# A graph layer whose one-hots get 128 columns: two columns of zeros, a later turning of fields, and parted sums of three rows

## The chip, the cores and the metric

The kernel runs on one core of one Trainium2 chip. The metric is the time of one execution on the device in microseconds (us). A core has five engines that run side by side and each take their instructions in order: PE (TensorE, the matmuls; its weight loads are shown as an engine of their own, PEld), DVE (VectorE), ACT (ScalarE), POOL (GpSimd, which also issues the gathers here) and SP (SyncE, which issues the plain DMAs).

## The reference

A graph with 625 nodes of 512 features and 20,625 edges, sorted by their destination, goes through one relational layer with four relations, and then through a feed-forward network:

```
h   = relu(layernorm(x))
msg = sum over r of (h[src] @ W_rel[r] + b_rel[r]) * where(edge_type == r, edge_weight, 0)
agg = segment_sum(msg, dst) / max(segment_sum(edge_weight, dst), 1)
x1  = layernorm(h + h @ W_self + b_self + agg) * g1 + b1
out = x + layernorm(x1 + gelu(x1 @ W_ffn1 + b_ffn1) @ W_ffn2 + b_ffn2) * g2 + b2
```

All inputs and the output are 32-bit floats; indices are 32-bit integers.

## The kernel before

The nodes are five blocks of 125 (`NG = 125`, padded to 128). The kernel has three stages.

**Table stage.** `table_rows(r, i)` makes one table row: block `i` of `h` times `W_rel[r]` (L366, four matmuls, each of which the profile shows as two records of 512 columns), scaled by ACT (L374) and written to a table in HBM by SP (L376). There are 4 x 5 = 20 such rows, in the order `(r, i)`, and 20 chunks of the table, so called. The last nine chunks (`KEPT = 9`) also stay in SBUF.

**Weights of dense blocks.** Three of the five blocks (`OUTER`) get their sums as a product: for each node of the block the edge weights are summed over (relation, source node), which gives a matrix `sums_w`, and this is multiplied with the table (L1043, one matmul for each of 20 chunks and each block; chunks that didn't stay come back from HBM as tiles `tr`, L1038). A node has up to 64 slots for edges. The slots' fields are turned by PE (`turn_fields`, L597) and copied by ACT (L600). They are taken in 12 units of 16 slots (`units`: 3 blocks x 4). For a unit, `slot_hots` makes one-hots on DVE: `low` (L614; which of the 125 source rows, and one more column that is always one), `eq` (L617) and three `high` (L620; which chunk, times the weight split in three bf16 parts). `slot_sums` then makes a *bank*: for each of four slots PE loads a piece of `low` as weights and multiplies it with a piece of `high` of 120 columns (L631). `empty_sums` (DVE, L637) adds the three parts of a bank into `sums_w`. So a unit is four banks, and all is 48 banks, or 192 weight loads and matmuls.

In memory `low` is laid out with the index of the slot inside (`TB = 8`), so that neighbouring columns of one weight load lie eight bf16 elements, 16 bytes, apart.

The first units are handled between the table rows: from a row given in the loop a unit is taken whenever few banks are waiting (`EARLY` units in all), and up to three banks (`PER_ROW`) are put behind each later table row. These rows are emitted in a fixed order by hand.

**Gather stage.** The rest is ordered by a planner (`Plan`): every operation has an engine, an estimated duration, what it comes after, buffers that it takes and gives back, and a rank; the planner plays this through and emits the instructions in the order it finds, so each engine's order is fixed when the kernel is built. In this stage are the units that are left, the products with the table, `h @ W_self` (L386), and the edges of the two blocks that aren't dense: POOL gathers 69 tiles of 128 table rows (L919, eight buffers `ms`) and four more (L973), with a pause behind every fourth (L915). Three gathered tiles make one sum: ACT writes the first, weighted, into a PSUM bank (L925; two banks, `add`), DVE adds the second and the third (L943). Then PE multiplies it with a one-hot. A *whole* sum does this with one 32-bit matmul (L966, two records). A *parted* sum is split into two halves of a shorter format, the high half by ACT (L929) and the low half by DVE (L933), and takes two short matmuls (L963, L964). Which sums are parted is said by

```
PARTED = 1, 2
def parted(k, units):
    return k % PARTED[1] < PARTED[0] and k + 3 < len(units)
```

so before it is every second one, except near the end of a group of sums.

**Tail.** Each block is normalised, turned (L319) and put through the feed-forward network (L714 up, L732 down); three blocks come last.

Of the kernel before, what the change touches and what calls it, by code (L numbers as in the profile page):

```python
# [12 lines left out]
BF16 = mybir.dt.bfloat16  # L13
# [3 lines left out]
P = 128  # L17
# [119 lines left out]
def gnn_layer(ctx, tc, x, edges, edge_groups, firsts, fourths, windows, w_self, w_rel, w_ffn1, w_ffn2, brel_in, rows_in, bf1_in, out, n_edges):  # L137
# [12 lines left out]
    nc = tc.nc  # L150
# [10 lines left out]
    NG = ep.each  # L161
# [7 lines left out]
    SL = windows.shape[1] // 4  # L169
# [11 lines left out]
    mid = ctx.enter_context(tc.tile_pool(name="mid", bufs=1))  # L181
# [89 lines left out]
    TB = 8  # L271
    TP = 2
# [1 line left out]
    grid = mid.tile([P, NG, TB], BF16, name="grid")  # L274
    keys = mid.tile([P, 2 * NC, TP], BF16, name="keys")
    ident_b = early.tile([P, P], BF16, name="ident_b")
    lows = [mid.tile([P, SL // 4 // TB, NG + 1, TB], BF16, name=f"low_{n}") for n in range(2)]

    def node_constants():
        place = early.tile([P, 1], F32, name="place")  # L280
        nc.gpsimd.iota(place, pattern=[[0, 1]], base=0, channel_multiplier=1, allow_small_or_imprecise_dtypes=True)
        nc.gpsimd.memset(node_f, 2.0 * N)
        nc.gpsimd.memset(xw, -1.0)
        for b in range(NB):
            n = ep.size[b]
            nc.vector.tensor_scalar(node_f[:n, at_of[b]:at_of[b] + 1], place[:n], float(ep.first[b]), None, op0=ALU.add)
            if b in inner:
                nc.vector.tensor_scalar(xw[:n, 0, b - B0:b - B0 + 1], place[:n], float(b * P), None, op0=ALU.add)
        nc.gpsimd.iota(keys, pattern=[[1, 2 * NC], [0, TP]], base=0, channel_multiplier=0,
                       allow_small_or_imprecise_dtypes=True)  # L290
        for t in lows:
            nc.gpsimd.memset(t[:, :, NG:, :], 1.0)
        nc.gpsimd.iota(grid, pattern=[[1, NG], [0, TB]], base=0, channel_multiplier=0,
                       allow_small_or_imprecise_dtypes=True)

# [37 lines left out]
    def pre_norm(i, mean):  # L333
        for c in (slice(0, D // 2), slice(D // 2, D)) if i == 0 else (slice(0, D),):
            nc.vector.tensor_scalar(z[:, i, c], xs[:, i, c], mean, 0.0, op0=ALU.subtract, op1=ALU.max)
        nc.vector.tensor_scalar(rx[:, i, 0:1], var_of[i], EPS, None, op0=ALU.add)
        rsqrt_pow(rx[:, i, :])
# [3 lines left out]
    def x_stats(i):  # L341
        st = work.tile([P, 2 if i == 0 else 1, 6], F32, tag="bn", name=f"st_x{i}", bufs=HOTS)
        w = D // st.shape[1]
        for h in range(st.shape[1]):
            nc.vector.bn_stats(st[:, h, :], xs[:, i, h * w:(h + 1) * w])
        mv = work.tile([P, 2], F32, tag="mv", name=f"mv_x{i}", bufs=HOTS)
        nc.vector.bn_aggr(mv, st)
        var_of[i] = mv[:, 1:2]
        return mv[:, 0:1]
# [240 lines left out]
    QT = 4  # L590
    UNIT = SL // 4
# [31 lines left out]
    def slot_sums(d, u, q, low, high, place):  # L623
        if (d, u, q) == (d, 0, 0):
            sums_w[OUTER[d]] = const.tile([P, NC, P], F32, tag="sums_w", name=f"sums_w{d}", bufs=2)
        pool, tag = place
        p = pool.tile([P, D], F32, tag=tag, name=f"bank_{d}_{u}_{q}")
        W = 3 * 2 * NC
        for i in range(QT):
            t = q * QT + i  # L630
            nc.tensor.matmul(p[:NG + 1, i * W:(i + 1) * W], low[:, t // TB, :, t % TB], high[:, t // TP, :, t % TP],  # L631
                             start=True, stop=True)
        return p

# [160 lines left out]
    PAUSE = 200  # L795
    RUN = 4
    LATER = 0.3
    PARTED = 1, 2
    LA = 3
    CH = 2  # L800
    FIRST_AT = (2, 3)
    units = [(d, u) for d in range(ND) for u in range(SL // UNIT)]
    EARLY = 7
    PER_ROW = 3
    with tc.manual_schedule(engines={PE, DVE, ACT, mybir.EngineType.Pool}):
        nc.scalar.activation(gelu_of, ones, AF.Gelu)
        node_constants()
        stats = x_stats(0)

        def next_norm(i):  # L810
            nonlocal stats
            if i < NB:
                pre_norm(i, stats)
            if i + 1 < NB:
                stats = x_stats(i + 1)

        warm = ps_one.tile([P, D], F32, tag="one", name="warm")
        for _ in range(WARM):
            nc.tensor.matmul(warm, zeros[:, :P], zeros, start=True, stop=True)
        next_norm(0)  # L820
        for k, n in ((0, 1), (1, 1), (2, 2)):
            transposed(hT[0][:, k:k + n, :], z[:, 0, k * P:(k + n) * P], f"h0_{k}")
        next_norm(1)
        hots, waiting, later, sums_now = {}, units[:EARLY], [], []
        for r in range(R):
            for i in range(NB):
                def next_transposed():
                    transposed(hT[i + 1], z[:, i + 1, :], f"h{i + 1}")
                    next_norm(i + 2 if i == 0 else i + 3)

                table_rows(r, i, next_transposed if r == 0 and i + 1 < NB else None)
                for d, u, q in sums_now:
                    p = slot_sums(d, u, q, *hots[d, u], ((ps_one, "one"), (ps_acc, "acc"), (ps_add, "add"), (ps_add, "add"))[q % 4])
                    empty_sums(d, u, q, p)
                sums_now = [later.pop(0) for _ in range(min(PER_ROW, len(later)))]
                if r == 0 and i < 3:
                    if i == 0:
                        next_norm(3)
                        find_tiles()
                    rows_of_tiles(2 * i, min(2 * i + 2, NB))  # L840
                if (r, i) == (0, 3):
                    find_windows()
                if (r, i) == (1, 0):
                    edge_columns()
                if (r, i) == (1, 1):
                    slot_weights(0, ND)
                    slot_fields()
                if (r, i) == (1, 4):
                    slot_weights(ND, NB)
                    slot_degrees()  # L850
                    degrees_turned = relation_degrees()
                if (r, i) == (2, 2):
                    degrees_turned()
                if (r, i) >= (1, 3) and waiting and len(later) + len(sums_now) <= UNIT // QT:
                    d, u = waiting.pop(0)
                    if d not in turned_fields:
                        turn_fields(d)
                    hots[d, u] = slot_hots(d, u)
                    later += [(d, u, q) for q in range(UNIT // QT)]
                if (r, i) == (1, NB - 1):  # L860
                    group_columns()
                if r == 3 and i < KD:
                    nc.vector.tensor_add(ws_sb[:, i, i * P:(i + 1) * P], ws_sb[:, i, i * P:(i + 1) * P], ident)
                if (r, i) == (3, 0):
                    for g_bc in (g1_bc, g2_bc):
                        nc.vector.tensor_scalar(g_bc, g_bc, 1.0 / RS, None, op0=ALU.mult)
                if (r, i) == FIRST_AT:
                    first_edges()
                    load_first_edges()
                if (r, i) == (2, NB - 1):  # L870
                    set_limits(0)
                    set_limits(1)
                    total_outside = count_outside()
            later_loads(r)
        assert not waiting
        for d, u, q in sums_now + later:
            p = slot_sums(d, u, q, *hots[d, u], ((ps_one, "one"), (ps_acc, "acc"), (ps_add, "add"), (ps_add, "add"))[q % 4])
            empty_sums(d, u, q, p)
        for d in range(ND):
            if d not in turned_fields:  # L880
                turn_fields(d)
# [53 lines left out]
    def parted(k, units):  # L935
        return k % PARTED[1] < PARTED[0] and k + 3 < len(units)

# [45 lines left out]
    g_last, g_before, n = None, None, 0  # L983
# [62 lines left out]
    m, ld, t, here = {b: None for b in OUTER}, None, None, {}  # L1046
    summed, h, e = {}, None, None

    def weights_of(d):
        nonlocal h, e  # L1050
        for i, (dd, u) in enumerate(units):
            if dd != d or i < EARLY:
                continue
# [12 lines left out]
    stay, i = list(range(NC - KEPT, NC)), 0  # L1066
    for d, b in enumerate(OUTER):
        weights_of(d)
        order = (*stay, *range(NC - KEPT)) if d != 1 else (*range(NC - KEPT), *stay)
        for c in order:  # L1070
            if c not in stay and (b, c) not in here:
                n = min(CH, NC - KEPT - c)
# [8 lines left out]
            if i == 8:  # L1081
                t = op("PE", 0.1, lambda: total_outside(), after=[m[b], first_ready], take=["ps"], give=["ps"], lag=2.0, rank=(2, 2.085))
# [15 lines left out]
    for b in range(NB):  # L1098
# [3 lines left out]
        for name, eng, us, fn, needs in steps:  # L1102
# [4 lines left out]
        p = [None]  # L1107
        t = op("PE", 0.46, lambda got=got, p=p, b=b: p.__setitem__(0, turn(got["x1"], f"x1_{b}")),
               after=[made["x1"]], take=["ps"], give=["ow"], rank=(1,))
# [5 lines left out]
    for blocks in together:  # L1115
        members, n = [], 0
# [177 lines left out]
```

## Time and profile before

| | before |
|---|---|
| time, median of 3 runs | 303.15 us (300.43 to 304.28) |
| profiled execution: time | 304.07 us |
| profiled execution: span of the trace | 302.2 us |
| mean granted TensorE clock | 0.977 |
| PE busy | 283.5 us (94%) |
| DVE busy | 188.5 us (62%) |
| POOL busy | 102.3 us (34%) |
| ACT busy | 60.1 us (20%) |
| moved by DMA | 47.94 MB |

The span runs from the first to the last instruction of the core, and the time of an execution has a little around it: 304.07 - 302.2 = 1.87 us here. Busy times are of the engine itself. A "group" of instructions is those of one line, engine, operation and shape, with their busy time and the mean of one in nanoseconds, and behind the bar the idle time of the engine just before them and what ended it. The chain is the work that ended last, followed back from the end; its pieces are exclusive, so that pieces on PE in a row give PE's true pace.

### The profile page before, as it was taken

What the parts mean: (1) busy time and instruction counts of PE and PEld (TensorE: products, weight loads), DVE (VectorE), ACT (ScalarE), POOL (GpSimd) and SP (SyncE); (2) the same over time, 40 slices, a digit from 0 to 9 for tenths busy, and PEclk for the clock granted to TensorE, in tenths of its full rate; (3) what the DMA queues carried; (4) which work ended last, traced back from release to release, by engine and by line L of the source; (5) the groups of instructions that cost most, each with busy time, mean ns of one, the idle gap of its engine ahead of it and who ended that gap; (6) DMA issues with size and microseconds to landing.
All of it is one profiled execution on the core that took longest, in us unless ns stands there. A gap on an engine that the chain in (4) does not pass through costs nothing.

```text
span 302.2 us, 3190 instructions
## 1 busy us (share of the span) xinstructions
PE 283.5 (94%) x1047; PEld 174.3 (58%) x1047; DVE 188.5 (62%) x440; ACT 60.1 (20%) x115; POOL 102.3 (34%) x146
## 2 busy tenths in 40 slices
PE   7999949999999999999697979999999999999991
PEld 3444414776677575644263745685954456686870
DVE  5613179677594678974686739697979650650614
ACT  2331120111210020212021202032532001121230
POOL 6161500000300008777777474742777110000000
PEclk9999987999999999999999979999999999999997
DMA  7759765852111139668999998551567332001011
GB/s 236 293 150 342 252 210 216 313 206 63 39 36 50 49 110 282 176 170 221 297 258 291 286 257 242 150 170 35 152 193 196 120 100 72 2 0 34 2 36 37
DMA packets 19972, 47.94 MB, mean 159 GB/s; under 512 B 2351, under 2 KB 3065, under 8 KB 19824
## 3 DMA queue, kind: packets, MB, share of 16 engines
q1 hardware_dynamic: 13348, 27.54, 28.1%
q0 software_dynamic: 6304, 19.89, 23.2%
q10 hardware_dynamic: 300, 0.26, 0.4%
q8 instruction: 9, 0.15, 0.2%
q14 instruction: 11, 0.09, 0.1%
HBM read 41.29 MB, written 6.52 MB: 158 GB/s over the span
## 4 chain that ended last, share of the span: by engine, by line
PE 73%; DMA 12%; DVE 6%; issue 4%; POOL 3%; SPq 1%; DVEq 0%; POOLq 0%
PE acc L1043 14%; PE pt L366 14%; PE bank L631 12%; PE pu L714 12%; PE po L732 11%; PE pz L386 5%; DMA tr<-table 4%; DMA ms<-table,row_i 4%; PE acc L966 3%; DMA xs<-in_x_dram 2%; DMA win<-in_windows_dram,at_i 2%; POOL dst L462 2%; PE acc L960 1%; POOL win L462 1%; PE acc L964 1%
## 5 line engine op out<-in xcount | busy, mean ns | idle before, releaser
L919 POOL DMA_INDIRECT ms<-table,row_i x69 | 69.0, 1000 | 70.6 <-DVE eq L617 33.7
L366 PE MATMUL pt<-wr,hT 128*128 128x512 f32 x160 | 74.4, 614 | 0.2
L631 PEld LDWEIGHTS <-low 128*126 128x126 bf16 x192 | 48.5, 321 | 9.9 <-issue 6.4
L637 DVE TENSOR_REDUCE sums_w<-bank 126x160 f32<-126x480 f32 x48 | 31.2, 656 | 30.7 <-PE bank L631 30.7
L366 PEld LDWEIGHTS pt<-wr,hT 128*128 128x128 f32 x160 | 30.3, 197 | 33.3 <-issue 32.8
L631 PE MATMUL bank<-high,low 128*126 128x120 bf16 x192 | 44.3, 367 | 0.0
L714 PE MATMUL pu<-x1T,w_sb 128*128 128x125 f32 x320 | 37.8, 276 | 0.0
L714 PEld LDWEIGHTS pu<-x1T,w_sb 128*128 128x128 f32 x320 | 36.9, 192 | 1.4 <-issue 1.4
L1043 PE MATMUL acc<-tr,sums_w 126*128 126x512 f32 x66 | 32.7, 626 | 3.7 <-DMA tr<-table 3.7
L732 PE MATMUL po<-w_sb,gT 128*125 128x512 f32 (+2 forms) x96 | 35.7, 521 | 0.0
L925 ACT ACTIVATE ea<-ms,ed 128x512 f32<-128x512 f32 x23 | 15.9, 691 | 60.6 <-DMA ms<-table,row_i 33.4
L943 DVE SCALAR_TENSOR_TENSOR ea<-ms,wgt_g,ea 128x512 f32<-128x512 f32 x31 | 22.9, 747 | 8.0 <-DMA ms<-table,row_i 6.6
L374 ACT ACTIVATE m<-pt,rx 125x512 f32<-125x512 f32 x20 | 13.7, 687 | 70.5 <-PE pt L366 60.4
L732 PEld LDWEIGHTS po<-w_sb,gT 128*125 128x125 f32 x96 | 16.5, 188 | 15.2 <-issue 13.0
L1043 PE MATMUL acc<-m,sums_w 126*128 126x512 f32 x54 | 25.2, 596 | 0.0
L718 ACT ACTIVATE gT<-pu,bf 128x125 f32<-128x125 f32 x40 | 14.7, 366 | 46.2 <-PE pu L714 46.2
L1043 PEld LDWEIGHTS acc<-tr,sums_w 126*128 126x128 f32 x66 | 12.4, 199 | 16.3 <-issue 11.6
L740 DVE TENSOR_TENSOR y<-po,z 125x512 f32<-125x512 f32 (+2 forms) x6 | 3.6, 603 | 24.2 <-PE po L732 24.2
L386 PE MATMUL pz<-ws_sb,hT 128*128 128x512 f32 x40 | 18.1, 596 | 0.0
L1043 PEld LDWEIGHTS acc<-m,sums_w 126*128 126x128 f32 x54 | 10.0, 191 | 10.2 <-issue 10.1
L555 POOL DMA_INDIRECT x_edges<-in_edge_groups_dram,x_group x2 | 1.9, 944 | 41.2 <-DVE x_group L551 40.9
L620 DVE TENSOR_TENSOR high<-eq,turned 128x640 bf16<-128x640 bf16 x36 | 15.5, 487 | 0.4
(168 smaller groups left out, 243.2 us busy)
## 6 DMA issues: line engine op xcount, KB each, us to landing
tr<-table SPq DMA_DIRECT2D x15, 504.0 KB
table<-m SPq DMA_DIRECT2D x20, 250.0 KB
w_sb<-in_L_gnn_W_ffn_dram SPq DMA_DIRECT2D x2, 2048.0 KB
wr<-in_L_gnn_W_rel_dram SPq DMA_DIRECT2D x3, 1024.0 KB
rows<-in_rows_dram SPq DMA_DIRECT2D x1, 1536.0 KB
ms<-table,row_i POOLq DMA_INDIRECT x69, 4.1
ws_sb<-in_L_gnn_W_self_dram SPq DMA_DIRECT2D x1, 1024.0 KB
out_dram<-y SPq DMA_DIRECT2D x4, 224.0 KB
```

Source lines behind the costliest of these rows:

```text
L366: nc.tensor.matmul(p, hT[i][:, k, :], wr_sb[r][:, k, :], start=(k == 0), stop=(k == KD - 1))
L386: nc.tensor.matmul(p[0], hT[i][:, k, :], ws_sb[:, k, :], start=(k == 0), stop=(k == KD - 1))
L620: nc.vector.tensor_mul(high[:, :, a * 2 * NC:(a + 1) * 2 * NC, :], eq, pairs(2 + a))
L631: nc.tensor.matmul(p[:NG + 1, i * W:(i + 1) * W], low[:, t // TB, :, t % TB], high[:, t // TP, :, t % TP], start=True, stop=True)
L637: nc.vector.tensor_reduce(sums_w[OUTER[d]][:NG + 1, :, n0:n0 + 2 * QT].rearrange("p c (t h) -> p t h c", h=2), p[:NG + 1, :QT * 3 * 2 * NC ...
L714: nc.tensor.matmul(pu[:, :nn], w1_sb[:, k, f * P:(f + 1) * P], x1T_b()[:, k, :nn], start=(k == 0), stop=(k == KD - 1))
L718: nc.scalar.activation(box["gT"][:, f, :nn], pus[f][:, :nn], AF.Gelu, bias=bf1[:, f:f + 1])
L732: nc.tensor.matmul(po[h][:n, :w], box["gT"][:, f, at], w2_sb[:, f, c], start=(f == 0), stop=(f == KF - 1))
L919: nc.gpsimd.indirect_dma_start(out=ms[j], out_offset=None, in_=table[:, :], in_offset=bass.IndirectOffsetOnAxis(ap=row_i[:, j:j + 1], axis=0))
L925: nc.scalar.activation(box["sum"], ms[j], AF.Copy, scale=wgt[:, j:j + 1])
L943: nc.vector.scalar_tensor_tensor(to, ms[j], wgt_g[:, k, q - 1:q], box["sum"], op0=ALU.mult, op1=ALU.add)
L1043: nc.tensor.matmul(acc[b,], sums_w[b][:NG + 1, c, :], kept[(b, c) if (b, c) in kept else c][:NG + 1], start=first, stop=last)
```

## The change

1. The tiles `low` get 128 columns in place of 126. Columns 126 and 127 are set to zero by POOL once for each of the two tiles. Matmuls of a bank now write all 128 rows of the bank; `empty_sums` reads 126 of them as before.
2. The turning of the fields and the first unit's one-hots move from behind row (1, 3) to behind row (1, 4) of the table; the block of degrees moves from (1, 4) to (2, 0), its turning from (2, 2) to (2, 3), the search of first edges from (2, 3) to (2, 2). Six units are handled between the table rows in place of seven; the seventh goes to the planner.
3. Every sum of three rows is parted but the last three of each group of sums.

```diff
-    lows = [mid.tile([P, SL // 4 // TB, NG + 1, TB], BF16, name=f"low_{n}") for n in range(2)]
+    lows = [mid.tile([P, SL // 4 // TB, P, TB], BF16, name=f"low_{n}") for n in range(2)]
...
         for t in lows:
-            nc.gpsimd.memset(t[:, :, NG:, :], 1.0)
+            nc.gpsimd.memset(t[:, :, NG:NG + 1, :], 1.0)
+            nc.gpsimd.memset(t[:, :, NG + 1:, :], 0.0)
...
-            nc.tensor.matmul(p[:NG + 1, i * W:(i + 1) * W], low[:, t // TB, :, t % TB], high[:, t // TP, :, t % TP],
+            nc.tensor.matmul(p[:, i * W:(i + 1) * W], low[:, t // TB, :, t % TB], high[:, t // TP, :, t % TP],
                              start=True, stop=True)
...
-    PARTED = 1, 2
+    PARTED = 1, 1
...
-    FIRST_AT = (2, 3)
+    FIRST_AT = (2, 2)
...
-    EARLY = 7
+    EARLY = 6
...
-                if (r, i) == (1, 4):
+                if (r, i) == (2, 0):
                     slot_weights(ND, NB)
                     slot_degrees()
                     degrees_turned = relation_degrees()
-                if (r, i) == (2, 2):
+                if (r, i) == (2, 3):
                     degrees_turned()
-                if (r, i) >= (1, 3) and waiting and len(later) + len(sums_now) <= UNIT // QT:
+                if (r, i) >= (1, 4) and waiting and len(later) + len(sums_now) <= UNIT // QT:
```

## The prediction

> **What bounds the kernel now.** First the page: span, busy times and the chain by engine.
>
> ```profile
> span 302.2 us, 3190 instructions
> PE 283.5 (94%) x1047; PEld 174.3 (58%) x1047; DVE 188.5 (62%) x440; ACT 60.1 (20%) x115; POOL 102.3 (34%) x146
> PE 73%; DMA 12%; DVE 6%; issue 4%; POOL 3%; SPq 1%; DVEq 0%; POOLq 0%
> ```
>
> PE is busy for 94% and carries the chain, so what PE no longer does comes off the time until another engine takes over. Next the groups by form, for the banks (L631) and for the other matmuls with bf16 weights (L597).
>
> ```profile
> L631 PEld LDWEIGHTS <-low 128*126 128x126 bf16 x192 | 48.5, 321 | 9.9 <-issue 6.4 <-DVE low L614 0.2 <-DVE x_step L419 0.2
> L597 PEld LDWEIGHTS <-fields 128*128 128x128 bf16 x15 | 1.5, 121 | 5.5 <-DVE fields L515 3.6 <-DVE fields L521 0.7 <-DVE fields L522 0.5
> ```
>
> A load of 126 bf16 columns lasts 321 ns, one of 128 columns 121 ns. The chain in order of time gives PE's pace, and cuts the run into stages.
>
> ```profile
> 44.16 0.29 PE tf L597
> 44.44 9.47 PE pt L366 x16
> 53.91 2.59 PE bank L631 x12
> 56.50 3.49 PE pt L366 x8
> ...
> 80.07 0.28 PE tf L597 x5
> ...
> 102.83 3.49 PE pt L366 x8
> 106.32 3.52 PE bank L631 x16
> ...
> 115.32 0.74 PE bank L631 x4
> ...
> 224.52 0.24 PE acc L963
> 224.76 0.24 PE acc L964
> 225.00 0.86 PE acc L966 x2
> ...
> 243.10 5.15 PE acc L1043 x12
> 248.25 0.44 PE tp_x L319 x4
> 248.69 3.57 PE pu L714 x32
> ...
> 295.53 0.30 DVE y L740
> ```
>
> A table row costs 3.49 us. Twelve pairs of load and matmul in three banks cost 2.59, so 0.216 a pair; a bank alone between other work costs 0.74, since its first load hides behind the matmul before. The five pairs of L597, with 128 columns, cost 0.28: 0.056 a pair. The stages: to the first turning of fields (44.45), table stage to the last row (106.32), gather stage to the turning of block 4 (248.25), tail of feed-forward to 295.53, and 6.7 to the end.
>
> The windows give engines by stage (columns: length, then busy time and count for PE, PEld, DVE, ACT, POOL, granted clock, DMA share, GB/s).
>
> ```profile
> 38.00:42.60 4.60, 1.51 (x5) 0.38 (x3) 4.21 (x15) 0.69 (x1) 0.00 (x0) 1.00 0.40 137
> 42.60:49.50 6.90, 5.94 (x11) 2.47 (x11) 5.36 (x14) 0.84 (x2) 0.00 (x0) 0.51 0.86 313
> ...
> 106.30:248.20 141.90, 135.69 (x479) 81.85 (x478) 106.98 (x220) 28.77 (x53) 83.22 (x108) 0.99 0.69 196
> ```
>
> Around 40 us PE waits for the fields, and then runs for 6.9 us at half its clock (0.51). In the gather stage PE is busy for 135.7 of 141.9, DVE for 107.0.
>
> **The change part by part: loads of 128 columns.** The trace has no load of 128 columns that lie 16 bytes apart. From below: the pairs of L597, 0.056 each, so 0.22 a bank. From above: the load keeps its pace, 0.216 x 128/126 x 4 = 0.88 a bank. I take 0.24, near the lower end, because L597 is the only row with this number of columns and this type and has a matmul as long (128 columns against 120). Against it stands that its columns are neighbours. The Trainium skill, "TensorE: Matmul & The Clock Gate", section "Weight-path perf modes — Fast Weight Load (FWL) and DoubleRow", says that a faster load, in four groups of 32 columns, is used when there are 128 weights and the type isn't FP32, for columns with a step too, and that about a factor of two was measured; with half of 0.216 a bank would cost 0.43, and the sum below would end at 280. The same page's section "LDWEIGHTS (loading the stationary operand)" gives columns / 1.2 ns, an estimated 105 ns for 126 columns; the 0.216 here is twice that, which speaks for a cost of the step that may stay.
>
> The two more memsets on POOL write 32 elements a partition each.
>
> ```profile
> L292 POOL MEMSET low<- 128x16 bf16 x2 | 0.1, 101 | 0.0
> ```
>
> Two of half the size take 0.1 each, and POOL waits for DVE soon after: nothing, or 0.2 without that wait.
>
> **Fields turned a row later, one unit fewer.** In the order of the built kernel, row (1, 4) now stands ahead of the first turning. It runs in PE's wait (39 to 44.2) and takes 3.5 us out of the table stage. The half clock also goes if the wait shrinks, as it should, from about 4 us (4.60 - 1.51 and 6.90 - 5.94) to 1.8 (39.0 + 3.5 to 44.2): rows (1, 4) and (2, 0) took 9.47 where two rows cost 6.98, so 2.5; I take it, the other end is 0. ACT's copy of row (1, 4) now stands ahead of the copies of the turned fields, and copies wait for their buffer's table write:
>
> ```profile
> 41.20 0.69 ACT L374 ACTIVATE m<-pt,rx 125x512 f32<-125x512 f32 x1 [4.79 <-DMA table<-m]
> ```
>
> The next such wait can hold the fields' copies, and DVE's first one-hots behind them, by up to about 1 us; PE has a further row, (2, 1), to do meanwhile. Then the table stage after 44.45 holds ten rows (34.9), 22 banks (5.3) and 0.5 of turnings: 40.7. DVE must make a unit and reduce its banks meanwhile:
>
> ```profile
> L637 DVE TENSOR_REDUCE sums_w<-bank 126x160 f32<-126x480 f32 x48 | 31.2, 656 | 30.7 <-PE bank L631 30.7
> L620 DVE TENSOR_TENSOR high<-eq,turned 128x640 bf16<-128x640 bf16 x36 | 15.5, 487 | 0.4
> L614 DVE TENSOR_TENSOR low<-turned,grid 128x2000 bf16<-128x2000 bf16 x12 | 14.3, 1193 | 1.8 <-ACT turned L600 1.8
> L617 DVE TENSOR_TENSOR eq<-turned,keys 128x640 bf16<-128x640 bf16 x12 | 5.8, 485 | 0.0
> L933 DVE TENSOR_TENSOR el<-ea,eh 128x512 fp32r<-128x512 f32 x8 | 5.5, 683 | 0.7 <-ACT eh L929 0.7
> ```
>
> A unit is 1.2 + 0.5 (eq) + 3 x 0.49, with overlap about 2.9, and a bank 0.6: for three banks, a row's worth, 4.0, against PE's 3.49 + 0.72 = 4.2. DVE follows closely, and stepping through both orders PE waits once, for PSUM banks of the first two units, for 1.5. The last row ends at 44.45 + 40.7 + 1.5 = 86.6 in place of 106.32: 19.7 less. This is the largest term, and some 14 of it hang on the loads.
>
> **Gather stage.** PE's work there: 24 banks at about 0.78 (between 0.74 and 0.86) become 26 at 0.24, -12.5; seven whole sums become parted, 0.86 to 0.48, -2.7; five chunk products (4.3), a turning and an eighth of an up-product (1.3) are now ordered ahead of the turning of block 4, +5.6. So 135.7 - 9.6 = 126.1. DVE gets one unit (2.9), two reductions (1.2) and seven low halves (0.68 each, 4.8): 107.0 + 8.9 = 115.9. ACT gets seven high halves of 0.58, 4.1 on top of 28.8: hidden, since it idles for 113; were it full, 4.1.
>
> ```profile
> L929 ACT CAST eh<-ea 128x512 fp32r<-128x512 f32 x8 | 4.7, 584 | 10.5 <-DVE ea L943 7.5 <-PE acc L963 2.9
> L943 DVE SCALAR_TENSOR_TENSOR ea<-ms,wgt_g,ea 128x512 f32<-128x512 f32 x31 | 22.9, 747 | 8.0 <-DMA ms<-table,row_i 6.6 <-ACT ea L925 1.2
> ```
>
> POOL's gathers:
>
> ```profile
> 112.74 1.25 POOL L919 DMA_INDIRECT ms<-table,row_i  x1 [33.70 <-DVE eq L617]
> ...
> 143.12 0.95 POOL L919 DMA_INDIRECT ms<-table,row_i  x1 [0.16 <-issue]
> ...
> 148.86 1.04 POOL L919 DMA_INDIRECT ms<-table,row_i  x1 [0.44 <-DMA ms<-table,row_i]
> ...
> 234.05 0.95 POOL L919 DMA_INDIRECT ms<-table,row_i  x1 [0.16 <-issue]
> ```
>
> They start 6.4 after the last table row and end, in issue, 14.2 before block 4 is turned; four with their pause take 5.74, so 73 need about 103. That makes 123.6 for the stage; the rest up to 141.9, 18.3, is POOL waiting for buffers. So POOL bounds the new stage between 123.6 (no waits) and 141.9 (the old ones), PE from below with 126.1, DVE between 115.9 and 153.7 (at its old share of 0.754). I take 135: the waits below go with the faster banks, but DVE has 8.9 more to do and no engine has much room.
>
> ```profile
> DVE sums_w L637 <- PE bank L631: 16.9, 13, 4.5
> ACT ea L925 <- DVE es L943: 13.2, 4, 6.0
> ```
>
> **Sum.** The tail loses the 5.6 that moved: 248.25 to 295.53 is 47.3, now 41.7, and 6.7 to the end. Span 86.6 + 135 + 41.7 + 6.7 = 270.0. With the 1.9 around a span, 271.9 against the profiled 304.07; that execution stood 0.9 above the median of the runs, so 271.0. With 126.1, no wait in the table stage and 0.22 a bank it would be 259; with 141.9, 278, and with the half clock kept 2.5 more: 259 to 281.
>
> **The rivals.**
> *The loads stay slow* (the change doesn't do what it says): the 16 bytes between columns cost, not their number. For: the only fast bf16 loads have neighbouring columns. Against: 32-bit loads of 128 columns keep up with pairs of 0.11 (3.57 / 32). Then the table stage holds 34.9 + 22 x 0.87 + 0.5 and ends at 99, the gather stage is 126.1 + 26 x 0.54 and the old 6.2 of idling = 146.3, and the span 293.7: 295.
> *DVE sets the gather stage*: it keeps its share of 0.754, because each half waits for ACT and each reduction for PE; 115.9 / 0.754 = 153.7. Span 288.7: 290. Against: 16.9 of its waiting was for banks.
> *Slower: two PSUM banks for all sums.* A parted sum keeps its bank through ACT's and DVE's further passes; if it is kept h us, 23 sums take 23h / 2, and this decides from about 11 us, and costs more than the kernel before from some 14.5. With 16 the stage is 184 and the time 320. For: ACT already waited 13.2 for such banks, 6.0 once. Against: the work on a bank is about 3.5 us (ACT's copy of a row, 0.69 as at 41.20, two of 0.75, 0.58, 0.68).
>
> **How the numbers follow.** Forecast 0.64, slow loads 0.18, DVE 0.13, slower 0.05. About 2% is what a measurement can tell; 295 is at that edge (297), so a bit over half of slow loads counts as faster, the rest as same: faster 0.64 + 0.13 + 0.10 = 0.87, same 0.08, slower 0.05. The range reaches from the floor to the middle of slow loads, 259 to 295; the forecast's own is 259 to 281.
>
> **What would show it.** Right: a pair of L631 under 0.08 in the chain, loads near 121 ns; no half clock near 45 us; last table row near 87; block 4 turned near 222; DVE over 80% busy between. Wrong: loads still over 300 ns; or the last row early but block 4 turned after 240, with PE idle behind DVE, POOL or `tr`.

## The result, and the profile after

The changed kernel took 278.88 us (median of 4 runs, 275.27 to 280.25) beside 302.6 us for the kernel before on the same chip: 0.9148 of its time, with a 95% interval of 0.9017 to 0.9279. On another chip it was run anew: 275.15 us (6 runs, 274.41 to 282.78) beside 301.26, which is 0.9149, from 0.9103 to 0.9195. So it is faster by 8.5%. (Medians are over all runs; ratios leave out the slow ones, which took over 1.5% longer than the fastest of the same kernel. Kernels that ran on different chips are compared by ratio.)

The page of the changed kernel: span, busy times, chain by engine.

```profile
span 276.3 us, 3214 instructions
PE 254.9 (92%) x1047; PEld 142.6 (52%) x1047; DVE 190.6 (69%) x447; ACT 63.9 (23%) x122; POOL 103.5 (37%) x148
PE 62%; DMA 12%; POOL 8%; issue 8%; DVE 6%; SPq 1%; ACT 0%; DVEq 0%; POOLq 0%
```

PE lost 28.6 us of work and the span 25.9; PE's share of the chain fell from 73% to 62%, and POOL's and "issue" grew. The groups by form (L632 is L631 of the kernel before):

```profile
L632 PEld LDWEIGHTS <-low 128*128 128x128 bf16 x192 | 17.2, 147 | 18.1 <-issue 17.8 <-DVE x_step L418 0.2
L638 DVE TENSOR_REDUCE sums_w<-bank 126x160 f32<-126x480 f32 x48 | 29.9, 649 | 7.5 <-PE bank L632 6.7
```

A load went from 321 ns to 147, and DVE's idle time behind the banks from 30.7 us to 6.7. The chain in order of time:

```profile
47.00 9.63 PE pt L367 x16
56.63 0.74 PE bank L632 x12
57.38 3.49 PE pt L367 x8
...
86.95 3.50 PE pt L367 x8
...
136.50 0.24 PE bank L632 x4
...
228.09 0.44 PE tp_x L320 x4
...
269.75 0.30 DVE y L741
```

Twelve pairs of load and matmul take 0.74 us in place of 2.59, so 0.062 a pair in place of 0.216. The last table row ends at 90.45 (before 106.32), block 4 is turned at 228.09 (248.25), and 41.7 us later `y` follows. The two rows behind the first turning still take 9.63 us, most of it at half clock (the granted clock is the third number from the end, here the mean over the window):

```profile
42.60:49.50 6.90, 3.76 (x8) 1.64 (x9) 5.29 (x14) 1.53 (x3) 0.00 (x0) 0.71 1.00 390
```

Of two profiled executions only this one shows it. DVE's work on the windows, which leads to the fields, began at 40.70 in it (first line below), since the gathers of the windows started 2.6 us later (the first at 31.67 in place of 29.07); in the second profiled execution of the same kernel it began at 37.86, and PE waited 0.62 us for the fields in place of 2.33:

```profile
40.70 0.35 DVE L494 CAST ends<-win 128x192 f32<-128x192 int32 x1 [6.64 <-DMA win<-in_windows_dram,at_i]
44.42 0.23 PE L598 MATMUL tf<-ident_b,fields 128*128 128x128 bf16 x1 [2.33 <-DVE fields L516]
```

```profile
37.86 0.35 DVE L494 CAST ends<-win 128x192 f32<-128x192 int32 x1 [6.40 <-DMA win<-in_windows_dram,at_i]
43.28 0.23 PE L598 MATMUL tf<-ident_b,fields 128*128 128x128 bf16 x1 [0.62 <-DVE fields L522]
43.97 7.10 PE L367 MATMUL pt<-wr,hT 128*128 128x512 f32 x16
```

There the sixteen matmuls take 7.10 us at full clock.

### The profile page after: what moved, and what is told of

The parts are those of the page before. It is cut to its first block, busy times and chain, and to the rows that moved or that the text cites. A ratio compares the mean times of both kernels' runs of the same rounds, so it can differ in the third digit from the quotient of the medians.

```text
span 276.3 us, 3214 instructions
## 1 busy us (share of the span) xinstructions
PE 254.9 (92%) x1047; PEld 142.6 (52%) x1047; DVE 190.6 (69%) x447; ACT 63.9 (23%) x122; POOL 103.5 (37%) x148
## 4 chain that ended last, share of the span: by engine, by line
PE 62%; DMA 12%; POOL 8%; issue 8%; DVE 6%; SPq 1%; ACT 0%; DVEq 0%; POOLq 0%
PE pt L367 14%; PE pu L715 13%; PE po L733 12%; PE acc L1044 12%; POOL ms L920 5%; DMA tr<-table 5%; PE bank L632 3%; DMA ms<-table,row_i 3%; DMA xs<-in_x_dram 3%; PE acc L967 3%; DMA win<-in_windows_dram,at_i 2%; POOL dst L463 2%; PE pz L387 1%; PE acc L965 1%; PE acc L964 1%
## 5 line engine op out<-in xcount | busy, mean ns | idle before, releaser
L715 PEld LDWEIGHTS pu<-x1T,w_sb 128*128 128x128 f32 x320 | 37.5, 192 | 5.2 <-issue 5.1
L638 DVE TENSOR_REDUCE sums_w<-bank 126x160 f32<-126x480 f32 x48 | 29.9, 649 | 7.5 <-PE bank L632 6.7
L944 DVE SCALAR_TENSOR_TENSOR ea<-ms,wgt_g,ea 128x512 f32<-128x512 f32 x38 | 27.9, 747 | 10.4 <-DMA ms<-table,row_i 4.1
L375 ACT ACTIVATE m<-pt,rx 125x512 f32<-125x512 f32 x20 | 13.8, 688 | 56.8 <-PE pt L367 45.2
L632 PEld LDWEIGHTS <-low 128*128 128x128 bf16 x192 | 17.2, 147 | 18.1 <-issue 17.8
L1044 PEld LDWEIGHTS acc<-tr,sums_w 126*128 126x128 f32 x66 | 12.2, 198 | 14.9 <-issue 11.0
L632 PE MATMUL bank<-high,low 128*128 128x120 bf16 x192 | 17.5, 226 | 2.4 <-issue 1.3
L615 DVE TENSOR_TENSOR low<-turned,grid 128x2000 bf16<-128x2000 bf16 x12 | 14.3, 1190 | 1.3 <-ACT turned L601 1.3
```

What stands on the lines that cost most here:

```text
L632: nc.tensor.matmul(p[:, i * W:(i + 1) * W], low[:, t // TB, :, t % TB], high[:, t // TP, :, t % TP], start=True, stop=True)
L638: nc.vector.tensor_reduce(sums_w[OUTER[d]][:NG + 1, :, n0:n0 + 2 * QT].rearrange("p c (t h) -> p t h c", h=2), p[:NG + 1, :QT * 3 * 2 * NC ...
L715: nc.tensor.matmul(pu[:, :nn], w1_sb[:, k, f * P:(f + 1) * P], x1T_b()[:, k, :nn], start=(k == 0), stop=(k == KD - 1))
L944: nc.vector.scalar_tensor_tensor(to, ms[j], wgt_g[:, k, q - 1:q], box["sum"], op0=ALU.mult, op1=ALU.add)
L1044: nc.tensor.matmul(acc[b,], sums_w[b][:NG + 1, c, :], kept[(b, c) if (b, c) in kept else c][:NG + 1], start=first, stop=last)
```

## The experiments

**The parts, one at a time.** Four kernels on one chip, beside a kernel before of 301.94 us: the columns alone; everything but the columns; everything but the parting; everything but the order of rows.

```diff
# columns alone: the kernel before, and
-    lows = [mid.tile([P, SL // 4 // TB, NG + 1, TB], BF16, name=f"low_{n}") for n in range(2)]
+    lows = [mid.tile([P, SL // 4 // TB, P, TB], BF16, name=f"low_{n}") for n in range(2)]
...
# 126 columns: the kernel after with these lines taken back
# parted by half: the kernel after, and
-    PARTED = 1, 1
+    PARTED = 1, 2
# old rows: the kernel after, and
-    FIRST_AT = (2, 2)
+    FIRST_AT = (2, 3)
-    EARLY = 6
+    EARLY = 7
...
```

Columns alone. 

> The kernel before with the 128 columns alone. Theory (the loads carry the gain): in the table stage some 22 banks fall from about 0.87 to 0.24 us, 14 us, and in the gather stage 24 banks by 0.54 make PE 13 us shorter, of which the other engines let through at least half; 302.6 less 20 to 25, so 278 to 283 us. Rival (the later turning and the parted sums carry a large part, as they give the engines the room that the faster loads need): the table stage gains its 14 and the gather stage next to nothing, 288 to 291.

Measured 281.48 us (279.75 to 283.6), 0.9332 of before, 0.9262 to 0.9402: the theory.

126 columns. 

> The kernel after with 126 columns again; the order of the rows and the parted sums stay. Theory: a pair of load and matmul takes 0.216 us again, the last table row ends near 103 (90.45 and 20 banks by 0.62), the gather stage is PE's again at about 142 to 146, so 295 to 299 us. Rival (order and parting are worth something by themselves): 290 or less.

Measured 295.1 us (293.79 to 295.79), 0.9811, 0.9751 to 0.9871. In its chain

```profile
44.30 6.97 PE pt L366 x16
51.28 2.59 PE bank L631 x12
```

the pair is at 0.216 us again, and the two rows are at full clock, as in the second execution above. The time is at the theory's lower end. The other two parts are worth something by themselves, 1.9%, with an interval (1.3 to 2.5%) that leaves open whether it is more than 2%.

Parted by half. 

> The kernel after, with only every second of the sums of three rows parted, as before. Theory (PE is the nearest bound of the gather stage, 128.2 of 137.7 us busy): seven whole sums cost PE 2.7 more and spare DVE 4.8 and ACT 4.1; 0 to +2.7 us, so 279 to 281. Rival (DVE sets the pace at 115.5 of 137.7): 2 to 5 us faster, 274 to 277.

Measured 284.05 us (282.5 to 286.59), 0.9445, 0.9344 to 0.9546. Neither held: it is slower, by more than the terms give.

Old rows. 

> The kernel after, with the rows of the table ordered as before: fields turned ahead of row (1, 4), seven units in the table stage. Theory: row (1, 4) leaves PE's wait for the fields and comes into the table stage, +3.5; the seventh unit there puts 2.2 us of DVE's units and banks ahead and takes the same from the gather stage; PE waits for DVE in the table stage for some of it. Together +1 to +4 us, so 280 to 283. Rival (the wait for the fields hides nothing, since the half clock and DVE set the stage): 277 to 279.

Measured 285.95 us (283.19 to 286.78), 0.9469, 0.9382 to 0.9556: slower than the theory's upper end.

So the columns alone bring 6.7% and the other two parts without the columns 1.9%, together the 8.5% of the whole change. But either of the other two, put on top of the columns without its fellow, brings nothing: 0.9469 and 0.9445 against 0.9332. (The whole change did not run on this chip; its 0.9148 and 0.9149 come from two others.) The windows from the last table row to `y` show where that lies (columns as in the prediction; kernels in the order after, after anew, columns alone, 126 columns, parted by half, old rows):

```profile
90.40:269.70 179.30, 169.78 (x760) 101.66 (x758) 129.99 (x280) 44.00 (x88) 83.74 (x108) 0.99 0.55 162
```
```profile
86.05:266.70 180.65, 172.67 (x759) 103.03 (x757) 130.06 (x281) 43.97 (x88) 82.37 (x108) 0.97 0.57 161
```
```profile
91.50:275.20 183.70, 174.09 (x752) 102.25 (x749) 121.63 (x266) 40.36 (x81) 83.60 (x108) 0.97 0.55 159
```
```profile
98.50:285.30 186.80, 181.64 (x760) 118.11 (x758) 130.50 (x280) 43.96 (x88) 85.54 (x108) 0.99 0.54 156
```
```profile
86.60:275.70 189.10, 175.31 (x759) 103.04 (x757) 125.81 (x273) 40.30 (x81) 85.06 (x108) 0.97 0.55 154
```
```profile
92.30:277.70 185.40, 173.22 (x752) 103.00 (x750) 125.65 (x273) 44.25 (x88) 84.14 (x108) 0.96 0.55 157
```

Length less PE's busy time is PE's idle time: 9.5 and 8.0 in the two executions after, 9.6 with the columns alone, 5.2 with 126 columns, and 13.8 and 12.2 in the two mixed kernels. The first figure of each row is where the table stage ended: 91.50 with the columns alone, 14.8 earlier than before. Parted by half, the table stage ends as early as in the kernel after run anew (86.60 and 86.05), and all of the 8.5 us follow later: 2.6 as PE's busy time and 5.8 as idle time, its longest piece here:

```profile
216.88 1.13 PE L967 MATMUL acc<-es,oh 128*128 128x512 f32 x2 [2.99 <-DVE es L944]
```

That is a whole sum of three rows, late near the end of the stage. PE waits for table chunks for only 1.1 us in this kernel, against 5.6 in the kernel after run anew; its waits are for sums and their halves (4.1 for whole sums, 2.5 for low and 1.8 for high halves). With the old rows the table stage is 6.3 longer (row (1, 4) and the half clock behind the wait for the fields), and PE waits 6.8 us for table chunks, late in the stage too, and once 3.1 for a high half:

```profile
218.71 2.08 PE L1044 MATMUL acc<-tr,sums_w 126*128 126x512 f32 x2 [3.18 <-DMA tr<-table]
```

The order of the gather stage is planned anew for each of these kernels, so which waits appear changes with the plan. Why these two plans leave more waits than the plan after is not separated by these runs.

**The kernel after, anew; PE's wait filled; no pauses.** Three kernels on one chip, beside a kernel before of 301.26 us.

```diff
# filled wait, ahead of the first turning of fields
+    busy = ps_one.tile([P, D], F32, tag="one", name="busy")
+    for _ in range(14):
+        nc.tensor.matmul(busy, zeros[:, :P], zeros, start=True, stop=True)
# no pauses
-    RUN = 4
+    RUN = 1000
```

After anew. 

> The kernel after, run anew. Undoing the parting alone or the order of rows alone (284.05 and 285.95 us) cost 5 to 7 us against its 278.88, which no sum of durations gives. Theory (the three edits fit together: with one undone PE stands still longer in the gather stage and then runs at half clock): 276 to 280 us again; PE's wait for the first fields near 0.6 us as in the two other kernels with this order of rows, so no half clock at 45 us and the last table row near 87. Rival (the first execution was a lucky order of events): 282 or more, with two or more stretches of half clock behind the last table row.

Measured 275.15 us, 0.9149 (0.9103 to 0.9195). The wait for the fields, the clock and the last row (86.05) are as the theory said. But the gather stage is not free of half clock:

```profile
137.86 1.92 PE L1044 MATMUL acc<-tr,sums_w 126*128 126x512 f32 x2 [2.54 <-DMA tr<-table]
```

PE waits for a table chunk until 137.86, and then its clock is half for 3.4 us, from 138.05 to 141.46. There are three such stretches, 10.2 us in all, as much as behind the last table row in the kernels parted by half and with the columns alone, so the clock of 0.97 is the same in the three. What sets the mixed kernels apart is idle time more than the clock; that half of the theory fell.

The traces show more of the half clock than the theory asked. Read in steps of 0.1 us, the other two stretches here run from 103.91 to 107.33 and from 148.29 to 151.70: each of the three lasts 3.41 us, and their starts are 10 and 3 times 3.41 apart. In the fourteen traces of this case, without the first 24 and the last 8 us, all 30 stretches last 3.41 or 6.83 us, and those of one trace lie on one such grid. So the clock seems to be set for a whole cell of the grid, 3.41 us, by what PE did in the cell before. Two cells, each with the one behind it, of the kernel after run anew and of the kernel before (the first busy time is PE's):

```profile
134.63:138.04 3.41, 0.87 (x3) 0.18 (x2) 2.82 (x8) 0.35 (x2) 2.32 (x4) 1.00 0.99 297
138.04:141.46 3.42, 3.42 (x9) 1.72 (x10) 2.39 (x8) 1.03 (x2) 2.86 (x5) 0.50 1.02 297
```
```profile
145.01:148.42 3.41, 1.49 (x4) 0.87 (x5) 2.70 (x5) 0.00 (x0) 2.74 (x5) 1.00 1.01 264
148.42:151.84 3.42, 3.42 (x9) 1.51 (x8) 2.18 (x5) 1.32 (x3) 2.37 (x3) 1.00 0.96 337
```

The two waits are nearly as long, 2.54 and 2.52 us, but the first leaves PE busy for a quarter of its cell and is followed by half clock, and the second lies across two cells, leaves 0.44 and costs nothing more. Over all the traces, each of the 18 cells at full clock in which PE was busy for less than 0.4 is followed by one at half clock; of those between 0.4 and 0.6 it is 8 of 27, of the busier ones 4 of 914, which this doesn't explain. That is read off the traces, and no run tests it.

Filled wait. 

> The kernel after with 14 more matmuls on zeros, 128x512 bf16, whose sum nobody reads, on PE ahead of the first turning of fields. Theory (the half clock from 45.5 to 52.3 follows from PE standing still before): the clock stays at 1.00 there, two table rows take 6.98 in place of 9.63; -2.7 us where PE waits 2.3, and up to +2 where the wait is 0.6 as in the trace of the kernel with 126 columns, since the fill then delays the fields. Rival (something else, such as the load on the chip, lowers the clock): half clock stays, 0 to +1.

Measured 276.72 us, 0.9168 (0.911 to 0.9225): no difference from the kernel after.

```profile
42.82 2.97 PE L861 MATMUL busy<-zeros 128*128 128x512 bf16 x13
...
45.91 7.08 PE L367 MATMUL pt<-wr,hT 128*128 128x512 f32 x16
```

(The trace has 13 of the 14 matmuls.) The clock stayed full, but in this execution DVE's work on the windows began early, at 38.49, as in the executions with this order of rows that kept the full clock without a fill; so the fill only delayed the turning, and the last row ended at 88.03, 2.0 after that of the kernel after anew. So this run doesn't tell the theory from its rival. Nearer to an answer is the spread over the other kernels: waits of 2.3 to 3.0 us here came with half clock (before, after, columns alone, old rows), single waits of 0.6 without (after anew, 126 columns, parted by half), though the kernel without pauses, below, ran at half clock behind two such waits.

No pauses. 

> The kernel after without POOL's pause behind each fourth gather. Theory (the gathers set the pace of the gather stage: 114.7 us from the first to the last after, 114.6, 115.0 and 116.1 in the three other kernels with fast loads, whatever the rest did): 17 pauses of 0.55 us fall away, first to last takes 106 to 110, and the time falls by 3 to 7 us until PE, busy for 128 of 137.7, is in its way. Rival (PE's and DVE's order holds the buffers that POOL waits for): POOL waits longer instead, first to last stays above 113, time within 1.5 us.

Measured 278.8 us, 0.9274 (0.9222 to 0.9326): 1.4% slower than the kernel after on that chip. For the gathers it is the rival's picture, but the rival allowed 1.5 us of time and it is 3.7. First and last gather without pauses, and of the kernel after anew:

```profile
95.63 1.60 POOL L920 DMA_INDIRECT ms<-table,row_i  x1 [27.11 <-DMA tr<-table]
...
209.60 0.95 POOL L920 DMA_INDIRECT ms<-table,row_i  x1 [0.30 <-issue]
```
```profile
93.42 1.62 POOL L920 DMA_INDIRECT ms<-table,row_i  x1 [26.64 <-DMA tr<-table]
...
209.46 0.95 POOL L920 DMA_INDIRECT ms<-table,row_i  x1 [0.44 <-issue]
```

114.0 us in place of 116.0: of some 9 us of pauses, 7 came back as waits for buffers. The gathers follow the consumers; their own pace is not what bounds the stage. Why the time grew is not shown: the profiled execution took 276.19 us, the shortest of the six, and its 2 us on the gathers are offset by a first gather 2.2 later.

**Why the load became fast.** The kernel after with neighbouring columns (2 bytes apart), once with 126 columns and once with 128; and the kernel after with 288 unused pairs behind the last table row, each kind eight times.

```diff
# neighbouring columns
-    TB = 8
+    TB = 1
# pairs of each kind (rows of zeros at steps of 2, 4, 8 bytes; one-hots at 16)
+    by_2, by_4 = (zeros.rearrange("p (c s) -> p c s", s=s) for s in (2, 4))
+    for n in (128, 127, 126, 124, 120, 112, 96, 64, 32):
+        for k in range(8):
+            nc.tensor.matmul(mix[:n, :120], zeros[:, k:k + n], zeros[:, :120], start=True, stop=True)
+        ...
```

126 neighbouring columns. 

> The kernel after with 126 columns again and with neighbouring columns in the one-hots (2 bytes apart in place of 16). Theory (the number of columns decides): a pair of load and matmul takes 0.21 to 0.22 us, a load about 320 ns, as with the step. Rival (the step decides): 0.06 to 0.11 us a pair and loads under 200 ns. DVE's one-hots are written in another order and may take longer, so the whole time is not read.

```profile
L631 PEld LDWEIGHTS <-low 128*126 128x126 bf16 x192 | 17.2, 143 | 21.5 <-issue 20.0 <-DVE high L620 0.9 <-DVE ends L493 0.2
L614 DVE TENSOR_TENSOR low<-turned,grid 128x2000 bf16<-128x2000 bf16 x12 | 26.8, 2234 | 1.3 <-ACT turned L600 1.3
```

The rival: 143 ns, with 126 columns. The number alone doesn't decide. DVE pays for it, 2234 ns a low one-hot in place of 1190 (281.21 us in one run).

All kinds. 

> The kernel after with 288 more pairs of load and matmul behind the last table row, eight in a row of each kind, whose sums nobody reads: 128, 127, 126, 124, 120, 112, 96, 64 and 32 columns, each with a step of 2, 4, 8 and 16 bytes between columns (four source lines). The rows so far: 126 columns at 16 bytes 0.216 us a pair and 320 ns a load, 126 at 2 bytes 143 ns, 128 at 16 bytes 147 ns. Theory (a load is fast when the step is 2 bytes or the number is 128, and slow otherwise): with 2 bytes every number is near 0.06 us a pair; with 4, 8 and 16 bytes 128 alone is, and 127 and below take 0.2 us or in proportion to their number. Rival (a number that is a multiple of 32 is enough): 96, 64 and 32 are fast with every step too. Second rival (the slowness comes with 16 bytes alone): 4 and 8 bytes are fast with every number.

The chain gives eight pairs of a kind per row: L880 is a step of 2 bytes, L882 of 4, L884 of 8, L886 of 16. First 128 columns, then 126 and 96:

```profile
87.17 0.42 PE mix L880 x8
87.59 0.42 PE mix L882 x8
88.01 0.42 PE mix L884 x8
88.43 0.51 PE mix L886 x8
...
92.72 0.46 PE mix L880 x8
93.19 0.48 PE mix L882 x8
93.67 0.93 PE mix L884 x8
94.60 1.85 PE mix L886 x8
...
107.02 0.42 PE mix L880 x8
107.44 0.42 PE mix L882 x8
107.86 0.71 PE mix L884 x8
108.57 1.42 PE mix L886 x8
```

With 128 columns the step costs next to nothing. Below 128 the time of a load goes with step times number, from 4 bytes up: 1.85 us for 8 x 126 columns at 16 bytes is 1.84 ns a column, 0.93 at 8 bytes is half of that, and 0.48 at 4 bytes is nearly hidden behind the matmul, whose pace is 0.42; 2 bytes bring no more than that, 0.46. 127 columns behave as 126 (1.86 at 16 bytes). A multiple of 32 isn't enough (96 columns: 1.42, 1.85 ns a column), so that rival fell, and the second too: 8 bytes cost also. The theory missed 4 bytes, which it held for slow. (The time of this kernel, 299.15 us in one run, is not read.)

128 neighbouring columns. 

> The kernel after with neighbouring columns (2 bytes apart) and 128 of them. Theory (one of the two is enough for a fast load, both bring no more): 0.06 us a pair, loads of 140 to 150 ns, as with one of them; DVE's low one-hots take 2.2 us each in place of 1.19, as with 126 neighbouring columns. Rival (the two add up): loads under 100 ns.

```profile
L632 PEld LDWEIGHTS <-low 128*128 128x128 bf16 x192 | 13.8, 99 | 26.1 <-issue 24.4 <-DVE high L621 1.2 <-DVE ends L494 0.2
```

Loads of 99 ns: both together do shorten the load further, as the rival said, but it lies behind matmuls either way. The single run took 283.94 us on a chip where the kernel before took 306.12.

126 columns at 4 bytes. 

> The kernel after with 126 columns again, but 4 bytes apart in place of 16 (two tiles of a one-hot beside each other in place of eight). Theory (below 128 columns a load takes 0.92 us for eight times 126 columns at 8 bytes, half of the 1.85 at 16, and 0.48 at 4, where it hides behind the matmul): a pair takes 0.06 us as with 128 columns, so the padding to 128 is not needed; DVE's low one-hots decide: at 1.19 us each, as with 16 bytes, the time is that of the kernel after, 274 to 279; at 2.23, as with 2 bytes, 279 to 284. Rival (banks in the kernel, with its other work beside, need 128): pairs above 0.1 us and 285 or more.

```diff
# the kernel after with 126 columns, and
-    TB = 8
+    TB = 2
```

```profile
L631 PEld LDWEIGHTS <-low 128*126 128x126 bf16 x192 | 16.7, 138 | 17.7 <-issue 16.9 <-DVE before L496 0.2 <-DVE x_step L417 0.2
L614 DVE TENSOR_TENSOR low<-turned,grid 128x2000 bf16<-128x2000 bf16 x12 | 14.3, 1190 | 1.3 <-ACT turned L600 1.3
```

Measured 274.96 us (273.67 to 276.91), 0.9191 of its kernel before, 0.9103 to 0.928: as fast as the kernel after, without the two columns of zeros. The theory held in the kernel itself.

**The planner told that chunks land later.** Beside the last two, on the chip with 306.12 us before.

```diff
-                ld = op("SP", 0.3, ..., take=["tr"], lag=6.2, order=True,
+                ld = op("SP", 0.3, ..., take=["tr"], lag=9.0, order=True,
```

> The kernel after, its planner told that a table chunk lands 9.0 us behind its issue in place of 6.2, so that PE's products on chunks are ordered later. Theory (what is left in the gather stage is PE's wait for table chunks, 5.6 us in the last trace, and the half clock that follows such waits, 10.2 us long there, 5 us of time): half of both goes, 270 to 273 us. Rival (the gathers set the pace, and a wait removed is waited elsewhere): 274 to 278.

Measured 279.34 us, 0.9133 (0.9083 to 0.9183), which is the kernel after again. That is the second half of the rival; its first half, that the gathers set the pace, is what the run without pauses speaks against. In the profiled execution, the longest of the six at 281.89 us, the waits for chunks fell from 5.6 to 3.5 us, a new one took their place, and the half clock grew from 10.2 to 17.1 us:

```profile
189.08 5.40 PE L1044 MATMUL acc<-m,sums_w 126*128 126x512 f32 x8 [3.21 <-DVE z L979]
```

## Why the prediction was right

It said 271.0 us, 259 to 295; 278.88 and 275.15 were measured. Its steps, by the profile of the execution anew and of the first one:

- *A bank of four pairs costs 0.24.* Measured 0.24 (x4 at 136.50) and 0.062 a pair; a load takes 147 ns, not near the 121 that was named as a sign, but it is hidden behind the matmul. The reason for the choice, though, was only half of one: the row it leaned on (128 neighbouring columns) differed from the old loads in number and in step, and the runs show that either of the two would do. The Trainium skill, "TensorE: Matmul & The Clock Gate", section "Weight-path perf modes — Fast Weight Load (FWL) and DoubleRow", says that the faster load is used with 128 weights, for columns with a step too; the 16-byte loads of 128 columns here agree. Its factor of two doesn't: 0.216 to 0.062 is 3.5, since the old load paid for the step.
- *Table stage to 86.6.* 86.05 anew; 90.45 in the first execution: 2.5 more from the late windows and 2.65 from the half clock that came with them, and 1.3 less since the wait for PSUM banks, put at 1.5, hardly came (47.00 + 40.7 + 2.65 is 90.35 already). Anew that wait was 0.8 (0.68 and 0.16, behind DVE's reductions).
- *The half clock goes.* It does when the windows land in time, as in most of the kernels with this order of rows; the first execution had the other end, 2.65 lost.
- *Gather stage 135.* 137.6 and 139.0 (225.01 - 86.05). This is the term that was too small. PE's work was put at 126.1 and took 128.2 and 131.1, at clocks of 0.99 and 0.96: less half of the stretches of half clock, which are 3.4 and 10.2 us long there, 126.5 and 126.0. So the count of work was right, and what was left out is the half clock that can follow PE's waits, 1.7 to 5.1 us. DVE's 115.9 was 115.5. The idle time implied, 8.9, was 9.5 and 7.9.
- *Tail 41.7 and end 6.7.* 41.7 and 6.6.

By the profiled executions the span was 3.4 and 6.3 us longer than the 270.0 of the sum, all in these two places. The rest of the 4 to 8 us is that the prediction took 0.9 off for a profiled execution above its median, which didn't recur anew (275.19 beside 275.15), and that the first execution lay 0.75 below its median. Of the rivals, slow loads is the kernel with 126 columns: 295 was said, 295.1 measured, and its two terms came out too (table stage to 99, measured 98.5; gather stage 146.3, measured 145.2). DVE did not set the stage alone: it was busy for 115.5 of 137.7, over the 80% that the prediction named, idled for only 6.7 us of the whole run behind the banks, and sparing it the seven low halves (parted by half) made the kernel slower. It is not far from its limit, though: with 126 columns, some 12 us more of its work (2 bytes against 4) came with 281.21 us in place of 274.96, in one run and on another chip. The rival of two PSUM banks didn't come. Not foreseen was how the other two parts go together: the prediction priced the parting at 2.7 of PE's work and gave the later turning its gain in the table stage alone, while undoing either costs about 3% of the time: without the parting 2.6 us of PE's busy time and 5.8 of its waits behind the table stage, without the later turning 6.3 us in the table stage (3.5 and the half clock were priced there) and 4.8 behind it.

## What to carry to other kernels

Look at how the columns of a weight tile lie before its matmuls are blamed: with 96 to 127 columns a step of 8 or 16 bytes made the load the pace of a bf16 matmul of 120 columns, and either 128 columns or a step of 4 bytes hid it, the second without padding. When an order is planned, price an edit in the planned order, not by its own durations: two edits that together brought 2% on top of the columns (0.915 against 0.933) were each worth nothing without the other. And read the granted clock behind every PE wait of some 2 us, since the wait can be paid again there.

## What the runs showed that was not expected

- A load of 96 to 127 columns of bf16 weights takes about 1.84 ns a column at 16 bytes and half at 8; at 128 columns the step has no such cost (0.42 to 0.51 us for eight pairs at any step).
- Half clock came in stretches of 3.41 us or twice that, on a grid, and each 3.41 us takes about 1.7 us of PE's work away. A wait of 2.54 us brought one, a wait of 2.52 that lay across two cells brought none. The Trainium skill, "TensorE: Matmul & The Clock Gate", section "HAM oscillation — how this bites in real kernels", tells to keep PE from idling for more than about 3.4 us; here less was enough, the 2.54 us.
- Taking away POOL's pauses made the kernel 1.4% slower, though the gathers took 2 us less from first to last; they wait for their consumers, and what made it slower stays open.
